# A recommender's attention pass: rows gathered straight from the embedding table instead of a prepared table of 128 columns

## The chip, the cores and the metric

One Trainium2 chip, of which the kernel uses one core. The metric is the device time of one execution in microseconds (us); lower is better. The kernel before takes 32778.58 us, the median of three runs (32776.94, 32778.58 and 32779.38 us). Engines are named as in the profile: PE is the matrix engine, DVE the vector engine, ACT the scalar engine, POOL the engine that issues the gathers, SP the engine that issues most other transfers.

## What is computed

The batch has B = 16384 samples; each has a history of L = 200 items, one candidate item, one category and one user. Rows of the embedding tables have D = 64 floats (256 bytes). All of it is 32-bit.

```
u, it, c = u_emb[user], i_emb[item], c_emb[cate]        # [B, 64] each
h = i_emb[hist]                                         # [200, B, 64]: 3.28 million rows
feat = concat([h, it, h - it, h * it])                  # [200, B, 256]
a = dice(feat @ au_W1 + au_b1, au_alpha, over the batch)# [200, B, 36]
w = a @ au_W2 + au_b2                                   # one weight per history row
cur = sum over the 200 of w * h                         # [B, 64]
z = concat([u, it, c, cur])                             # [B, 256]
z = dice(z @ W1 + b1);  z = dice(z @ W2 + b2);  out = z @ W3 + b3
```

`dice` takes mean and variance over the batch (for the attention: of each of the 200 positions by itself), and multiplies x by p + alpha (1 - p), where p is the sigmoid of the normalised x. Because the moments run over the batch, a position's weights can be formed only after all its 16384 samples have passed the first layer.

## The kernel before

The samples of one position l are cut into 128 columns of 128 samples, and the columns into ND = 8 chunks of TD = 16. One *step* k handles chunk k % 8 of position k // 8; there are 1600 steps. A step's work is spread over ten later steps, since the weights have to wait for the moments of the position.

**A prologue makes a table.** For each item it stores 128 floats in device memory: the row of `i_emb` and, beside it, the row's product with the first-layer weights (`blk_h`). `table_rows` and `table_store` do that block by block; meanwhile POOL gathers the candidate items, users and categories (384 gathers, `fetch_one`, `keep_one`); the users and categories are turned and stored to device memory (`ucT`) for the end.

**A step of the main part** (`step`, around L440) then does, in this order of issue: `fetch(k)` gathers 16 columns from the table on POOL, one gather of 128 rows of 512 bytes each (L144); an addend `xit` is loaded by SP (L344); `x_of(k-10)` goes through the sigmoid and a scaling on ACT (L423, L426); `turn(k-1)` transposes the landed rows on DVE (L354, four instructions of 64x1024); ACT copies the addend and the turned rows into PSUM (L428, L430); `hidden(k-2)` adds what the matmul made (L366) and measures it (L368); `product(k-1)` multiplies the rows with the items (L360) and multiplies by the weights `blk_m` on PE (L194, four matmuls of 512 columns); `weigh(k-10)` forms the weights by a product (L374), a transpose (L375), a reduction (L377) and three small instructions (L381, L384), multiplies the rows by them (L389) and adds to `cur` (L390). Once a position, `moments` makes mean and variance.

**One tile in 256 does not come by a gather.** In every sixteenth step (`has_side`) POOL gathers 15 columns, and the sixteenth column comes by address: SP reads 128 addresses into registers and issues one transfer of one row for each (`rows_by_address`, L332), 8 in each step, into a tile `side` that ACT copies into place (L349).

**What sets the order.** The loop (L459) has a body of LPB = 24 positions and runs 8 times; the last 8 positions follow without a loop. Each engine executes its instructions in the written order, and waits at an instruction until the others have done what it needs. `fetch(k)` overwrites the buffer of `fetch(k-12)`, so POOL waits for `weigh(k-12)`. At the end of each pass through the loop's body all engines meet.

**After the main part** the head runs by itself: the stored users and categories are loaded again (L512), the first layer takes two matrices of 80 outputs (L194 of `px`), then its dice (L528, L529, L535), the second layer, its dice, and the third layer with 256 narrow matmuls (L551) and one output transfer (L555).

Of the kernel before, what the change touches and what calls it, by code (L numbers as in the profile page):

```python
# [9 lines left out]
I32 = mybir.dt.int32  # L10
# [10 lines left out]
LPB = 24  # L21
LAND = 12
EVERY = 16
ROW = 4 * 2 * D
U8 = mybir.dt.uint8
EARLY = 4
IDX = 2
XI = 2
# [3 lines left out]
def din_kernel(  # L32
# [31 lines left out]
    Z1, Z2, ZO = W1.shape[1], W2.shape[1], W3.shape[1]  # L64

# [3 lines left out]
    dram = ctx.enter_context(tc.tile_pool(name="dram", bufs=1, space=bass.MemoryType.DRAM))  # L69
# [4 lines left out]
    def quarter(e, g, n=S):  # L74

        return slice((2 * e + g) * S, (2 * e + g) * S + n)


    eps = const.tile([P, 1], F32, name="eps")
    nc.vector.memset(eps, EPS)  # L80

    parts = [(0, S), (S, A - S)]

    blk_h = const.tile([P, P], F32, name="blk_h")
    blk_i = const.tile([P, P], F32, name="blk_i")
    blk_m = const.tile([P, P], F32, name="blk_m")
    au_w = const.tile([P, 4, A], F32, name="au_w")
    au_bias = const.tile([P, 1], F32, name="au_bias")  # L90
    au_al = const.tile([P, 1], F32, name="au_al")
    au_1al = const.tile([P, 1], F32, name="au_1al")
    au_w2 = const.tile([P, 1], F32, name="au_w2")
    au_bias2 = const.tile([P, 1], F32, name="au_bias2")
    for t in (blk_h, blk_i, blk_m, au_bias, au_al, au_w2):
        nc.vector.memset(t, 0.0)
    nc.sync.dma_start(au_bias2, au_b2.partition_broadcast(P))
    for e in range(2):
        rows = au_W1.rearrange("(g d) a -> d g a", d=D)[e * S : (e + 1) * S]
        for g in range(2):  # L100
            r = quarter(e, g)
            nc.sync.dma_start(au_w[r], rows)
            for q, (a0, n) in enumerate(parts):
                c, a = quarter(q, g, n), slice(a0, a0 + n)
                nc.vector.tensor_add(blk_h[r, c], au_w[r, 0, a], au_w[r, 2, a])
                nc.vector.tensor_sub(blk_i[r, c], au_w[r, 1, a], au_w[r, 2, a])
                nc.vector.tensor_copy(blk_m[r, c], au_w[r, 3, a])
    for g in range(2):
        for q, (a0, n) in enumerate(parts):
            r, a = quarter(q, g, n), slice(a0, a0 + n)  # L110
            nc.sync.dma_start(au_bias[r], col(au_b1)[a])
            nc.sync.dma_start(au_al[r], col(au_alpha)[a])
            nc.sync.dma_start(au_w2[r], au_W2[a])

    nc.vector.tensor_scalar(au_1al, au_al, -1.0, 1.0, ALU.mult, ALU.add)
    nc.vector.tensor_mul(au_1al, au_1al, au_w2)
    nc.vector.tensor_mul(au_al, au_al, au_w2)

    itT = const.tile([P, ND, CD], F32, name="itT")
    cur = const.tile([P, NT, D], F32, name="cur")  # L120
    nc.vector.memset(cur, 0.0)


    land = [const.tile([P, TD, 2 * D], F32, name=f"land{i}") for i in range(EARLY)]
    idx = [const.tile([P, NT], I32, name=f"idx{i}") for i in range(IDX)]

    side = [const.tile([P, 2 * D], F32, name=f"side{i}") for i in range(2)]
    addr = [const.tile([1, P], I32, name=f"addr{i}") for i in range(2)]
    stats = [const.tile([P, 2 * ND, nc.vector.BN_STATS_DIM], F32, name=f"st{i}") for i in range(2)]
    rstds = [const.tile([P, 1], F32, name=f"rs{i}") for i in range(2)]  # L130
    shifts = [const.tile([P, 1], F32, name=f"sh{i}") for i in range(2)]
    px = [psum.tile([P, CD], F32, name=f"px{i}") for i in range(2)]
    ph = psum.tile([P, CD], F32, name="ph")
    pg = psum.tile([P, CD], F32, name="pg")


    table = dram.tile([V, 2 * D], F32, name="table")
    xi = dram.tile([ND, P, CD], F32, name="xi")
    ucT = dram.tile([2, ND, P, CD], F32, name="ucT")

    def gather(dst, ids, rows):

        for n in range(ids.shape[1]):
            nc.gpsimd.indirect_dma_start(  # L144
                out=dst[:, n, :],
                out_offset=None,
                in_=rows,
                in_offset=bass.IndirectOffsetOnAxis(ap=ids[:, n : n + 1], axis=0),
            )

    def load_ids(t, ids):
        nc.sync.dma_start(t, ids.rearrange("(p n) -> p n", n=NT))

    def load_hist_ids(i, l):
        nc.sync.dma_start(idx[i], r_hist[ds(l, 1), :].rearrange("l (p n) -> p (l n)", n=NT))

    def load_addresses(m, l):

        t = addr[m % 2]
        with nc.allow_non_contiguous_dma(reason="one index of each partition"):  # L160
            nc.sync.dma_start(
                t.unsqueeze(1), r_hist[ds(l, 1), :].rearrange("l (p n) -> l n p", p=P)[:, NT - 1 :]
            )
        nc.vector.tensor_scalar_mul(t, t, ROW)  # L164

    def has_side(k):
        return k % EVERY == EVERY - 1

    def by_tile(t, i):

        return t[:, ts(i, CH)].rearrange("p (n t) -> p n t", t=S)

    def transpose(dst, rows, n=TD):

        for i in range(2):
            for e in range(2):
                nc.vector.transpose(
                    by_tile(dst[ts(e, D)], i)[:, :n], rows[ts(i, D), :n, ts(e, S)]
                )

    def transpose_back(rows, src, n=TD):

        for i in range(2):
            for e in range(2):
                nc.vector.transpose(
                    rows[ts(i, D), :n, ts(e, S)], by_tile(src[ts(e, D)], i)[:, :n]
                )

    def layer(dst, pairs, n=CH, onto=False):

        for i in range(2):
            cols = slice(i * CH, i * CH + n)
            for j, (lhsT, rhs) in enumerate(pairs):
                nc.tensor.matmul(  # L194
                    dst[:, cols], lhsT, rhs[:, cols],
                    start=(j == 0 and not onto), stop=(j == len(pairs) - 1),
                    skip_group_check=onto,
                )

    def scale_and_shift(mean, var, n, rstd=None, shift=None):  # L200

        std = small.tile([P, 1], F32, tag="std", name="std")
        nc.scalar.activation(std[:n], var, AF.Sqrt, bias=eps[:n])  # L203
        if rstd is None:
            rstd = small.tile([P, 1], F32, tag="rstd", name="rstd")
            shift = small.tile([P, 1], F32, tag="shift", name="shift")
        nc.vector.reciprocal(rstd[:n], std[:n])
        nc.vector.scalar_tensor_tensor(shift[:n], mean, -1.0, rstd[:n], ALU.mult, ALU.mult)
        return rstd[:n], shift[:n]


    with ExitStack() as start:
        pre = start.enter_context(tc.tile_pool(name="pre", bufs=3))
        ids = [start.enter_context(tc.tile_pool(name=f"ids{i}", bufs=1)).tile(
            [P, NT], I32, name=f"ids{i}") for i in range(3)]
        for t, v in zip(ids, (r_item, r_user, r_cate)):
            load_ids(t, v)
        load_hist_ids(0, 0)

        per = V // P  # L220
        rest = V - P * per
        grid = i_emb[: P * per].rearrange("(p n) d -> p n d", n=per)
        grid_out = table[: P * per].rearrange("(p n) d -> p n d", n=per)
        blocks = [(n0, min(TD, per - n0)) for n0 in range(0, per, TD)]
        if blocks[-1][1] == TD and rest:
            blocks.append((per, 0))
        tabs = {}

        def table_rows(b):

            n0, n = blocks[b]
            tab = pre.tile([P, TD, 2 * D], F32, tag="tab", name="tab")
            m = n
            if n:
                nc.sync.dma_start(tab[:, :n, :D], grid[:, n0 : n0 + n])
            if b == len(blocks) - 1 and rest:
                nc.vector.memset(tab[:, n, :D], 0.0)
                nc.sync.dma_start(tab[:rest, n, :D], i_emb[P * per :])
                m = n + 1
            rT = pre.tile([P, CD], F32, tag="rT", name="rT")  # L240
            transpose(rT, tab, m)
            layer(px[b % 2], [(blk_h, rT)], n=m * S)
            tabs[b] = tab, m

        def table_store(b):
            n0, n = blocks[b]
            tab, m = tabs.pop(b)
            transpose_back(tab[:, :, D:], px[b % 2], m)
            if n:
                nc.scalar.dma_start(grid_out[:, n0 : n0 + n], tab[:, :n])  # L250
# [335 lines left out]
```

## Time and profile before

| | us |
|---|---|
| median of three runs | 32778.58 |
| span of the profiled execution, first to last instruction | 32775.9 |
| POOL busy, 25888 instructions | 24422.0 (75% of the span) |
| DVE busy, 28939 instructions | 25619.7 (78%) |
| ACT busy, 7214 instructions | 7665.2 (23%) |
| PE busy, 7216 matmuls | 6395.0 (20%) |
| POOL's first gather begins | 9.80 |
| POOL's last gather begins | 32399.71 |

The profile is of one execution, taken by the hardware's profiler. A group's row gives the line, engine and operation, the tile written and those read, how often it ran, the busy time and the mean of one in ns, and after the second bar how long the engine was idle just before, with what ended the idle time. "issue" there means that the profile shows nothing that the engine waited for: it was the engine's own handling of the next instruction. In the timeline each row has its start, its length and, in brackets, the idle time before it. Share of busy time alone does not tell the bound: DVE and POOL have nearly the same.

### The profile page before, as it was taken

The page shows a single profiled execution, that of the slowest core. Times are in us where ns is not written, and L with a number is a line of the kernel's source. Part 1 is how long each engine was busy: PE and PEld are TensorE (multiplying, and loading weights), DVE is VectorE, ACT ScalarE, POOL GpSimd, SP SyncE. Part 2 cuts the span into 40 slices and gives each one's busy share as a digit, 9 for nine tenths or more (in the row PEclk, how much of TensorE's full clock was granted, in tenths as well). Part 3 has the DMA queues.
Part 4 walks back from the last instruction along what each step waited for, and adds up shares of the span by engine and source line. Part 5 has one row for each costly group of instructions (what it writes and reads, how often), then busy time and mean ns, then how long its engine had stood idle before and what let it go on. Part 6 is the DMA issues. An engine that isn't in the chain of part 4 may idle for free. (4 is left out here: it accounts for less than half of the span.)

```text
span 32775.9 us, 127799 instructions
## 1 busy us (share of the span) xinstructions
PE 6395.0 (20%) x7216; PEld 2044.0 (6%) x7216; DVE 25619.7 (78%) x28939; ACT 7665.2 (23%) x7214; POOL 24422.0 (75%) x25888
## 2 busy tenths in 40 slices
PE   3111111111111111111111111111111111111113
PEld 0000000000000000000000000000000000000001
DVE  7777777777777777777777777777777777777776
ACT  1222222222222222222222222222222222222222
POOL 7777777777777777777777777777777777777774
PEclk5555555555555555555555555555555555555555
DMA  5222222222222222222222222222222222222221
GB/s 157 80 80 80 80 79 80 79 80 79 80 80 80 80 78 80 80 80 80 79 80 80 79 80 80 80 80 80 79 79 80 80 80 78 80 80 79 80 80 53
DMA packets 1245023, 2650.84 MB, mean 81 GB/s; under 512 B 574678, under 2 KB 613622, under 8 KB 1237942
## 3 DMA queue, kind: packets, MB, share of 16 engines
q0 software_dynamic: 828288, 1685.41, 19.9%
q1 hardware_dynamic: 405238, 893.85, 8.8%
q10 hardware_dynamic: 10560, 63.79, 0.5%
q14 instruction: 922, 7.55, 0.1%
q8 instruction: 15, 0.25, 0.0%
HBM read 2577.29 MB, written 63.91 MB: 81 GB/s over the span
## 5 line engine op out<-in xcount | busy, mean ns | idle before, releaser
L144 POOL DMA_INDIRECT land<-table,idx x25500 | 24059.4, 944 | 7852.3 <-issue 7532.9
L354 DVE STREAM_TRANSPOSE hx<-land 64x1024 f32<-64x1024 f32 x6404 | 7938.0, 1240 | 5528.1 <-DMA land<-table,idx 5338.6
L194 PE MATMUL px<-hm,blk_m 128*128 128x512 f32 x6404 | 5974.7, 1088 | 25917.5 <-DVE hm L360 25917.5
L426 ACT ACTIVATE pg<-gate,au_al,au_1al 128x1024 f32<-128x1024 f32 x1610 | 1943.8, 1207 | 12867.9 <-DVE cur L390 12867.6
L430 ACT COPY ph<-hx 128x1024 f32<-128x1024 f32 x1601 | 1627.7, 1017 | 10549.5 <-DVE hx L354 10549.5
L194 PEld LDWEIGHTS px<-hm,blk_m 128*128 128x128 f32 x6404 | 1879.4, 324 | 30012.2 <-DVE hm L360 28357.9
L368 DVE BATCH_NORM_STATS2 st<-land 128x6 f32<-128x512 f32 x3204 | 2061.0, 685 | 55.0
L375 DVE STREAM_TRANSPOSE yT<-pg 128x1024 f32<-128x1024 f32 x1610 | 2011.8, 1250 | 55.2
L389 DVE TENSOR_TENSOR pg<-land,ph 128x1024 f32<-128x1024 f32 x1610 | 1977.7, 1228 | 54.9
L390 DVE TENSOR_TENSOR cur<-pg,cur 128x1024 f32<-128x1024 f32 x1610 | 1970.5, 1224 | 55.5
L377 DVE TENSOR_REDUCE r<-yT 128x32 f32<-128x1024 f32 x1610 | 1964.0, 1220 | 55.3
L366 DVE TENSOR_TENSOR land<-px,hx 128x1024 f32<-128x1024 f32 x1602 | 1961.6, 1224 | 49.5
L423 ACT ACTIVATE gate<-land,sh,rs 128x1024 f32<-128x1024 f32 x1610 | 1991.5, 1237 | 2.9
L374 DVE TENSOR_TENSOR pg<-pg,land 128x1024 f32<-128x1024 f32 x1610 | 1968.9, 1223 | 11.0 <-ACT pg L426 11.0
L360 DVE TENSOR_TENSOR hm<-ph,itT 128x1024 f32<-128x1024 f32 x1601 | 1932.0, 1207 | 5.6 <-ACT ph L430 5.6
L428 ACT COPY px<-xit 128x1024 f32<-128x1024 f32 x1601 | 1591.4, 994 | 31.8 <-PE px L194 22.0
L384 DVE SCALAR_TENSOR_TENSOR ph<-r,au_bias,r 64x16 f32<-64x16 f32 x3220 | 773.7, 240 | 114.8
L164 DVE TENSOR_SCALAR addr<-addr 1x128 int32<-1x128 int32 x100 | 31.2, 312 | 702.6 <-DMA addr<-in_r_hist 702.6
L423 ACT ACT_TABLE_LOAD x210 | 269.4, 1283 | 558.4 <-DMA land<-table,idx 333.0
L381 DVE COPY r<-r 64x32 f32<-64x32 f32 x1610 | 322.8, 200 | 55.0
L203 ACT ACT_TABLE_LOAD x203 | 260.4, 1283 | 3.5
L203 ACT ACTIVATE std<-var,eps 128x1 f32<-128x1 f32 x201 | 59.2, 294 | 721.0 <-DVE var L410 721.0
(79 smaller groups left out, 2102.9 us busy)
## 6 DMA issues: line engine op xcount, KB each, us to landing
xit<-xi SPq DMA_DIRECT2D x1601, 512.0 KB
land<-table,idx POOLq DMA_INDIRECT x25500, 2.5
side<-table SPq DMA_DIRECT2D x12800, 0.5 KB
table<-tab ACTq DMA_DIRECT2D x48, 1024.0 KB
tab<-in_L_rec_i_emb SPq DMA_DIRECT2D x48, 512.0 KB
idx<-in_r_hist SPq DMA_DIRECT2D x200, 64.0 KB
ucT<-t ACTq DMA_DIRECT2D x16, 512.0 KB
land<-ucT SPq DMA_DIRECT2D x16, 512.0 KB
```

Source lines behind the costliest of these rows:

```text
L144: nc.gpsimd.indirect_dma_start(out=dst[:, n, :], out_offset=None, in_=rows, in_offset=bass.IndirectOffsetOnAxis(ap=ids[:, n : n + 1], axis=0),
L194: nc.tensor.matmul(dst[:, cols], lhsT, rhs[:, cols], start=(j == 0 and not onto), stop=(j == len(pairs) - 1), skip_group_check=onto,)
L354: nc.vector.transpose(dst.rearrange("p s (n t) -> p n s t", t=S), rows[ts(i, D), :, :, e])
L366: nc.vector.tensor_add(x_of(k), by_row(px[k % 2]), by_row(hx[k % 2][:, 1]))
L368: nc.vector.bn_stats(stats[l % 2][:, 2 * c + i, :], x_of(k)[:, ts(i, TD // 2)])
L374: nc.vector.tensor_mul(by_row(pg), by_row(pg), x_of(k))
L375: nc.vector.transpose(yT, pg)
L377: nc.vector.tensor_reduce(r, yT.rearrange("p (i n u) -> p i n u", i=2, u=S), mybir.AxisListType.X, ALU.add)
L389: nc.vector.tensor_mul(by_row(pg), rows, w.unsqueeze(2).to_broadcast([P, TD, D]))
L390: nc.vector.tensor_add(cur[:, ts(c, TD)], by_row(pg), cur[:, ts(c, TD)])
L423: nc.scalar.activation(by_row(gate), x_of(k - 10), AF.Sigmoid, bias=shifts[i], scale=rstds[i])
L426: nc.scalar.activation(pg, gate, AF.Identity, bias=au_al, scale=au_1al)
```

## The change

Nothing of the result changes. What is done differently:

- **No table.** The prologue that multiplied all of `i_emb` and stored a table is gone. The gathers read `i_emb` itself, rows of 256 bytes, into `rows` (a ring of 5 tiles of 128x16x64; before, 12 of 128x16x128). The product with `blk_h` is formed in each step on PE, and the item's part too (`blk_i` with `itT`), so the addend `xit` and its transfers are gone.
- **All work in the turned layout.** `turn` transposes 64 instead of 128 floats per row into `hT` (four instructions of 64x512, as those of L177 before). The weight of a row is formed by a matmul with a matrix of ones per block (`blk_w`) that also spreads it over the row's 64 places; one instruction multiplies by the turned rows and one adds to `curT`. The transpose, reduction and small instructions of `weigh` are gone.
- **One column by address in each position.** `SIDES = (7,)`: chunk 7 of every position gathers 15 columns, and its sixteenth comes by address on SP, 16 rows in each step (25600 rows in all; before, 12800). The addresses are one contiguous load.
- **Users and categories last.** Of the 384 gathers outside of the history, 128 (items) stay at the beginning; 256 (categories and users, in turns) follow the last history gather, while the last ten steps' weighing still runs. The first layer of the head is done chunk by chunk beside these gathers (`head_layer`, from the third of these 16 steps on).
- **A new head.** Two groups of 64 samples side by side fill all 128 partitions; 64 of the 80 first-layer outputs go to `za`, the other 16 of four chunks share one tile `zb`. The third layer is 16 wide matmuls and two transposes, and eight output transfers (and one small) go out.
- **Loop.** The body holds 45 positions and runs 4 times; 20 positions follow without a loop.

The core of the diff ("..." where lines are left out):

```diff
-LPB = 24
-LAND = 12
-EVERY = 16
-ROW = 4 * 2 * D
+LPB = 45
+ROWS = 5
+LAG = 10
+XR = 9
+IDX = 3
+SIDES = (7,)
+LOAD = 16
+ROW = 4 * D
...
-    table = dram.tile([V, 2 * D], F32, name="table")
...
+    def transpose(dst, of):
+        for i in range(2):
+            for e in range(2):
+                nc.vector.transpose(by_tile(dst[ts(e, D)], i), of[ts(i, D), :, ts(e, S)])
...
+    def fetch(k):
+        l, c = divmod(k, ND)
+        for n in range(TD - has_side(k)):
+            j = column(c, n)
+            gather(rows[k % ROWS], idx[l % IDX][:, j : j + 1], n, i_emb)
+
+    def gate(k):
+        i = k // ND % 3
+        nc.scalar.activation(pg, xs[k % XR], AF.Sigmoid, bias=shifts[i], scale=rstds[i])
+        nc.scalar.activation(pg, pg, AF.Identity, bias=au_al, scale=au_1al)
+
+    def weights(k):
+        nc.vector.tensor_mul(y, pg, xs[k % XR])
+        layer(wb, [(blk_w, y)])
+
+    def weigh(k):
+        nc.vector.scalar_tensor_tensor(wb, wb, au_bias2, hT[k % LAG], ALU.add, ALU.mult)
+        nc.vector.tensor_add(curT[k % ND], wb, curT[k % ND])
+
+    def hidden(k):
+        nc.scalar.activation(xs[k % XR], px, AF.Identity, bias=au_bias)
+
+    def measure(k):
+        l, c = divmod(k, ND)
+        for i in range(2):
+            nc.vector.bn_stats(stats[l % 3][:, 2 * c + i, :], xs[k % XR][:, ts(i, CH)])
+
+    def turn(k):
+        if has_side(k):
...
+            nc.scalar.copy(rows[k % ROWS][:, TD - 1], side[m % 3])
+        transpose(hT[k % LAG], rows[k % ROWS])
+        layer(px, [(blk_h, hT[k % LAG]), (blk_i, itT[k % ND])], last=False)
+        nc.scalar.copy(ph, hT[k % LAG])
+
+    def product(k):
+        nc.vector.tensor_mul(hm, ph, itT[k % ND])
+        layer(px, [(blk_m, hm)], first=False)
...
+    def step(k, last=None):
...
+        if has(k):
+            fetch(k)
+        if has(k - LAG):
+            gate(k - LAG)
+            weights(k - LAG)
+        if has(k - 2):
+            hidden(k - 2)
+            measure(k - 2)
+        if has(k - 1):
+            turn(k - 1)
+        if has(k - LAG):
+            weigh(k - LAG)
+        if has(k - 1):
+            product(k - 1)
+        if has(k - 2) and (k - 2) % ND == ND - 1:
+            moments((k - 2) // ND)
...
+        load_ids(ids[0], r_item)
+        load_hist_ids(0, 0)
...
+        nc.gpsimd.iota(lanes, pattern=[[1, P]], base=P, channel_multiplier=-1)
+        attention_weights()
...
+        ask(-1, L)
+        head_weights()
...
+    with tc.manual_schedule():
+        steps(BODY, L - BODY, L - BODY)
+        for j in range(2 * ND + 2):
+            if j < 2 * ND:
+                head_fetch(K + j, j)
+            step(K + j, last=K - 1)
+            if 1 <= j <= 2 * ND:
+                transpose(ucT[(j - 1) % 4], rows[(K + j - 1) % ROWS])
+            if j >= 2:
+                head_layer(j - 2)
...
+        for c in range(ND + 1):
+            if c < ND:
+                dice(curT[c], za[c], na, al1a, ala)
...
+                    nc.tensor.matmul(pz[c % 4][:, cols], w2a, curT[c][:, cols], start=True, stop=False)
+                    nc.tensor.matmul(pz[c % 4][:, cols], w2b[q], ab[c // 4][q, cols], start=False, stop=True)
+            if c:
+                nc.scalar.activation(z2[c - 1], pz[(c - 1) % 4], AF.Identity, bias=bias2)
+                measure_head(2, c - 1, z2[c - 1])
```

In the built order `head_weights` (45 small transfers on SP and some small DVE work) stands, but for one memset, behind the loop, in the first two steps of the 20 positions that follow it.

## The prediction

> **What bounds the kernel now.** I read the groups first (the page's costliest groups), for the idle time as much as for the busy time.
>
> ```profile
> L144 POOL DMA_INDIRECT land<-table,idx x25500 | 24059.4, 944 | 7852.3 <-issue 7532.9
> L354 DVE STREAM_TRANSPOSE hx<-land 64x1024 f32<-64x1024 f32 x6404 | 7938.0, 1240 | 5528.1 <-DMA land<-table,idx 5338.6
> ```
>
> POOL and DVE are equally busy, but their idle times differ in kind. DVE waits 5339 us for gathered rows to land: it has time to spare. POOL's idle time is "issue": it waits for nobody, and needs about 0.3 us between gathers. Then the timeline: POOL alone around the end of a pass through the loop's body, the passage of the index load, and the last gather.
>
> ```profile
> 8147.89 0.94 POOL L144 DMA_INDIRECT land<-table,idx  x1 [0.30 <-issue]
> 8158.63 0.94 POOL L144 DMA_INDIRECT land<-table,idx  x1 [9.79 <-issue]
> ...
> 11975.98 0.94 POOL L144 DMA_INDIRECT land<-table,idx  x1 [0.30 <-issue]
> 11977.22 0.94 POOL L144 DMA_INDIRECT land<-table,idx  x1 [0.30 <-issue]
> 11987.96 0.94 POOL L144 DMA_INDIRECT land<-table,idx  x1 [9.79 <-issue]
> ...
> 32399.71 0.94 POOL L144 DMA_INDIRECT land<-table,idx  x1 [0.30 <-issue]
> ```
>
> From 8158.63 to 11977.22 lie one body's gathers, 24 x 128 less 12 = 3060, so 3059 intervals: 3818.59 / 3059 = 1.2483 us each, with no other gap. So POOL's gathers are the bound, from the first at 9.80 to the last at 32399.71: 25884 gathers (25500 and 3 x 128), 25883 intervals x 1.2483 = 32310, and the rest of the 32389.9 is 80 us of gaps. The gaps are seven turns of the loop (six of 10.74 - 1.25 = 9.5 us, the first, at 4321.87, of 6.2), 2.7 at its exit, and two waits of 9.7 and 4.4 for a buffer of the ring at 528 and 558. Preparing the table costs nothing today: it lies beside the first 384 gathers.
>
> After the last gather come 375.2 us (32400.65 to 32775.9) without POOL. The chain of waits that ended last shows what fills them.
>
> ```profile
> 32498.29 112.47 PE px L194 x256
> 32619.83 10.44 PE px L194 x12
> ...
> 32693.26 7.00 PE ph L551 x32
> 32703.63 7.00 PE pg L551 x32
> ```
>
> The ten delayed steps' weighing lasts until 32500, then follow the head's first layer (112 us), its second (until about 32690) and eight pieces of third layer, one each 10.37 us. So span = 9.8 + 32310 + 80 + 0.9 + 375.2 = 32775.9. The runs' median is 2.7 above this span, and I add 2.7 at the end.
>
> **The change, part by part.** *Price of a gather.* It reads 256 bytes instead of 512 per row, from `i_emb`, into a tile of 64 columns. The trace of before has such gathers: those of its prologue.
>
> ```profile
> L144 POOL DMA_INDIRECT land<-in_L_rec_i_emb,ids x128 | 120.9, 944 | 48.0 <-issue 38.1 <-DMA ids<-in_r_item 9.3 <-DMA land<-in_L_rec_i_emb,ids 0.6
> L144 POOL DMA_INDIRECT land<-table,idx x25500 | 24059.4, 944 | 7852.3 <-issue 7532.9 <-DMA land<-table,idx 123.1 <-DVE yT L375 66.4
> ```
>
> 944 ns for 64 columns, 944 ns for 128; issue 38.1 / 127 = 0.30 us in both. Halving the bytes gains POOL nothing and costs it nothing. The users' group of the same prologue has 128 gathers with 120.8 busy and 39.0 idle: 159.8 / 128 = 1.2484. I take 1.2483, and 0.001 to either side as bounds, so +-25 us.
>
> *Number of gathers.* 200 x 127 + 3 x 128 = 25784, which is 100 fewer: 100 x 1.2483 = -125 us. Intervals: 25783 x 1.2483 = 32185.
>
> *What must now keep up with POOL*, which needs 16 x 1.2483 = 19.97 us for a step. DVE, by rows of before: product for the weights 1.22 (L374), measuring 2 x 0.685 (L368), four 64x512 transposes x 0.706 = 2.82 (L177), weighing 2 x 1.22 (L389, L390 the nearest), product 1.21 (L360): 9.1 us against about 16.0 (25619.7 / 1600) before. ACT: 1.24 + 1.21 + 1.11 + 1.02 = 4.6. PE: eight matmuls x 1.09 = 8.7. In series from landing: transposes 2.8, weighing 2.4, product 1.2, two matmuls 2.2, ACT 1.1, measuring 1.3 = 11 us. None reaches 19.97, so the 7 us per step that DVE saves gain nothing, and the matmuls added cost nothing: POOL's issue hides them. `fetch(k)` now waits for the turning of k-5 instead of the weighing of k-12. POOL feels it only where a `turn` comes later than four steps of issue, 80 us, less landing and turning (1.64 from the last gather's end to L354 at the end of before, and 2.8): 75 us of cover. Behind a late gather the next turn waits, and behind that nobody who isn't already waiting. The two ring waits at 528 and 558 go (ring now freed after turning): -14, between -14 and 0.
>
> *Rows by address* on SP: 128 for each position instead of 64.
>
> ```profile
> 496.97 48.66 SPq L332 DMA_DIRECT2D side<-table  x124
> 552.32 2.73 SPq L332 DMA_DIRECT2D side<-table  x8
> 556.48 2.87 SPq L332 DMA_DIRECT2D side<-table  x8
> ```
>
> 124 rows in 48.66 us, register loads and all, are 0.39 us a row; in the loop 8 rows, an addend load and a register load take 4.16 us, at most 0.52 a row. So 50 to 67 us of SP's 158.5 us per position (127 x 1.2483), and the addend loads are gone. SP starts a position's rows eight steps before use, and the last 16 rows two steps before. Past them on SP's queue move the index load, the address load and, once, head_weights' 45 transfers (x 0.4 = 18 us, behind the loop); each is wanted no sooner than four steps (80 us) later, and the DVE instructions that wait on those 45 have the 75 us cover. Nothing, then. Here a rule speaks against the change: the Trainium skill, "DMA: Bandwidth & Descriptors", section "Anatomy of one DMA", gives a DMA a fixed cost of about 2 us whatever its size (stated for the path that POOL uses). If SP paid that in series, a position would take 128 x 2 = 256 us, SP would be the bound and the kernel would take 200 x 256 = 51200 us. The row says 0.39: the fixed part overlaps among transfers. I go by the row.
>
> A second rule: the skill, "SBUF — State Buffer", section "SBUF: two separate sides", says that a DVE instruction in a 2-port mode locks POOL out of writing descriptors, so that its DMAs wait until DVE is done. In the timeline near 15003 (DVE busy without pause) and 15013 (DVE idle for 7 us) the gathers have the same 0.94 and 0.30. DVE's forms after are those of before except the weighing's scalar_tensor_tensor, which has its output in PSUM. By the row: 0. By the rule, if that one form locked: up to 1600 x 1.2 = +1920 us.
>
> *Loop.* Three turns instead of seven: 3 x 9.5 + 2.7 at the exit = 31 us of gaps, between 25 and 45 (the body is longer; what an edge costs after it no row shows). With the ring waits gone, gaps go from 80 to 31.
>
> *Start.* The ids come first on SP. Before, the ids' transfer was issued at 7.84 and the first gather began at 9.80, so 2 us later; now issue at about 0.8 gives 2.8. POOL has an iota before it that no row shows: nearest are its own memsets, 0.1 us, and DVE's 128x128 memset, 0.17. I take a start at 4; bounds 2.8 and 12 (iota of 9 us).
>
> *After the last gather.* Users' gather lands and is turned: 1.6 + 2.8. Its first layer: four matmuls 4, ACT 1.1, measuring 1.3, so 11 us with hops. Two chains of moments: 3 each (of before: 32613.2 to 32615.0, with two more small matmuls), so 17. Table load 1.3, two dice (1.24, 0.8, 1.22) for `zb` and the first for `za`: 25. Second layer: four matmuls x 0.86 = 3.4 per chunk, DVE 0.8 + 1.22 + 1.29 = 3.3 per chunk; they alternate at about 3.8, so 8 x 3.8 = 31 and 3 for the last ACT and measuring: 59. Moments and table load 5: 64. Third: eight dice x 2.02 of DVE = 16, a transpose and two sums 1.7 twice, the last two matmuls 1.7, output 4 x 0.4 and 2.5 to land: 90. I take 90 against 375.2; bounds 75 and 120. The first layer and the ten steps' weighing lie beside the 256 gathers at the end; if that cover were gone, their 98 and 112 us come back, about 300.
>
> Sum: 4 + 32185 + 31 + 0.9 + 90 = 32311 span, + 2.7 = **32314 us**, 1.4% less: -125 gathers, -49 gaps, -6 start, -285 end.
>
> **The rivals.** *A, the tail isn't hidden.* The head's first layer needs `curT` complete; if weighing runs late it follows the gathers as before, with 200 to 300 us at the end: about 32480. Against it: DVE has 9 us of work in 20. *B, POOL waits once per position for the side column*, since chunk 7 now comes by address in each: a few us x 200; with 1 us 32514. It needs a `turn` 75 us late. *C, slower: POOL's gathers get dearer* through the weighing instruction's hold on the shared port (place: every step; price up to its 1.2 us). It decides from 465 / 25784 = 0.018 us per gather, 0.29 us per step; at half its length per step the result is 32314 + 960 = 33274. Against it: sixteen gathers a step at a constant 1.25 beside every form of before. *D, the gain is given back exactly* would need C's price at 0.29: hardly.
>
> **How the numbers follow.** Mine 0.87, A 0.03, B 0.04, C 0.05, D 0.01. My case's own range from the bounds (gathers +-25, gaps -6 to +14, start -1 to +8, end -15 to +30, not all at once) is 32275 to 32370, nine times in ten: 0.78. To hold 8 in 10 I go to 32270 and 32390. A measurement tells 0.2% (66 us) from no change; faster are mine, A and B: 0.94; same 0.01; slower 0.05.
>
> **What would show it.** POOL's gathers at 944 ns and 0.30 us apart, 25784 of them, idle mostly by "issue"; DVE busy about 14600 us and waiting longer for landing; SP's rows near 0.4 us; three gaps of about 10 us; a first gather before 5 us; 75 to 120 us after the last one. I am wrong if the interval isn't 1.248, if POOL waits on DVE, or if the end is longer.

## The result, and the profile after

The changed kernel takes **32351.83 us** (median of four runs, 32349.32 to 32352.71); the kernel before took 32778.98 beside it (four runs, 32776.94 to 32779.74). The ratio is 0.987, with a 95% interval of 0.9856 to 0.9884: 1.3% faster. The forecast was 32314 with a range of 32270 to 32390. The profiled execution has a span of 32350.9 us. This holds for a chip on which the kernel before takes 32779 us. Three other chips came up in the experiments, on which the kernel before needs 15% more; there all variants of the change that were run are slower than the kernel before, as the experiments tell. In the text TensorE is the profile's PE, VectorE its DVE, ScalarE ACT, GpSimd POOL and SyncE SP; the granted clock is the share of full speed at which TensorE's clock ran.

The costliest groups of the kernel after, with the row of the new weighing instruction and the count of each engine (columns: busy us, mean ns of one, idle us before, what ended most of it):

```profile
PE 15634.4 (48%) x26020; PEld 6232.0 (19%) x26020; DVE 14906.8 (46%) x18956; ACT 7799.0 (24%) x7281; POOL 24330.4 (75%) x25789
...
L117 POOL DMA_INDIRECT rows<-in_L_rec_i_emb,idx x25400 | 23967.5, 944 | 7767.4 <-issue 7296.0
L146 DVE STREAM_TRANSPOSE hT<-rows 64x512 f32<-64x512 f32 x6404 | 4519.2, 706 | 12357.6 <-DMA rows<-in_L_rec_i_emb,idx 11955.0
...
L286 DVE SCALAR_TENSOR_TENSOR wb<-wb,au_bias,hT 128x1024 f32<-128x1024 f32 x1610 | 2080.9, 1292 | 82.6 <-PE wb L151 30.4
```

DVE fell from 25619.7 to 14906.8 us, and what it saved became waiting: for landing rows it now waits 11955 us, 5339 before. POOL has the same 944 ns and the same kind of idle time, "issue". It is still the bound. The timeline of POOL, at the start and at one of the loop's edges (the end of a pass through its body):

```profile
0.86 0.22 POOL L379 IOTA lanes<- 128x128 int32 x1 [0.40 <-POOLq L538]
2.83 1.09 POOL L117 DMA_INDIRECT rows<-in_L_rec_i_emb,ids  x1 [1.75 <-DMA ids<-in_r_item]
...
14434.25 0.94 POOL L117 DMA_INDIRECT rows<-in_L_rec_i_emb,idx  x1 [0.30 <-issue]
14445.07 0.94 POOL L117 DMA_INDIRECT rows<-in_L_rec_i_emb,idx  x1 [9.87 <-issue]
```

The iota took 0.22 us, inside the wait for the ids. In the whole trace only four intervals between gathers are longer than 1.4 us: 4.88 at 7296, 10.82 at 14434 and at 21579, 3.72 at 28723. The two ring waits of before are gone. Less four normal intervals that makes 25.2 us of gaps.

The last gather ends at 32216.88, and the span at 32350.93: 134 us. The chain of work that ended last, in order of time (start, length, what), shows what fills them:

```profile
32215.93 2.31 DMA rows<-in_L_rec_u_emb,ids
...
32243.65 2.04 PE px L488 x2
32245.70 2.00 PE px L489 x2
...
32319.68 9.58 PE px L151 x16
...
32333.06 9.70 PE pg L151 x16
```

From 32243.65 to 32307.8 TensorE works on the second layer (L488, L489) without pause: 64 us. The third layer is the two pieces of 16 matmul instructions at L151. Stretches of this end by engine (columns: stretch, length, busy us and instructions of PE, PEld, DVE, ACT, POOL, then the granted clock, the DMA share and GB/s):

```profile
32235.00:32260.00 25.00, 16.34 (x17) 4.35 (x18) 11.11 (x12) 8.35 (x8) 0.00 (x0) 0.50 0.00 1
32260.00:32310.00 50.00, 47.80 (x48) 11.63 (x47) 18.44 (x24) 13.19 (x12) 0.00 (x0) 0.50 0.00 0
32310.00:32351.00 41.00, 20.39 (x36) 8.79 (x36) 20.62 (x29) 12.21 (x11) 0.00 (x0) 0.67 0.02 3
```

In the second row TensorE is busy 47.80 of 50 us at a granted clock of 0.50, with 48 instructions: 1.00 us each.

### The profile page after: what moved, and what is told of

The parts are those of the page before. It is cut to its first block, busy times and chain, and to the rows that moved or that the text cites. A ratio compares the mean times of both kernels' runs of the same rounds, so it can differ in the third digit from the quotient of the medians.

```text
span 32350.9 us, 170467 instructions
## 1 busy us (share of the span) xinstructions
PE 15634.4 (48%) x26020; PEld 6232.0 (19%) x26020; DVE 14906.8 (46%) x18956; ACT 7799.0 (24%) x7281; POOL 24330.4 (75%) x25789
## 5 line engine op out<-in xcount | busy, mean ns | idle before, releaser
L117 POOL DMA_INDIRECT rows<-in_L_rec_i_emb,idx x25400 | 23967.5, 944 | 7767.4 <-issue 7296.0
L151 PE MATMUL px<-hT,blk_h 128*128 128x512 f32 x6404 | 5638.3, 979 | 15307.4 <-DVE hT L146 15307.4
L146 DVE STREAM_TRANSPOSE hT<-rows 64x512 f32<-64x512 f32 x6404 | 4519.2, 706 | 12357.6 <-DMA rows<-in_L_rec_i_emb,idx 11955.0
L151 PEld LDWEIGHTS px<-hT,blk_h 128*128 128x128 f32 x6404 | 1808.7, 313 | 18318.3 <-issue 17505.7
L151 PE MATMUL px<-itT,blk_i 128*128 128x512 f32 x6404 | 4721.2, 830 | 0.0
L151 PE MATMUL wb<-y,blk_w 128*128 128x512 f32 x6440 | 3412.6, 656 | 1253.6 <-DVE y L282 1253.6
L295 DVE BATCH_NORM_STATS2 st<-xs 128x6 f32<-128x512 f32 x3204 | 2058.3, 684 | 3695.9 <-ACT xs L290 3695.9
L151 PE MATMUL px<-hm,blk_m 128*128 128x512 f32 x6408 | 3037.0, 596 | 38.9 <-DVE hm L382 35.0
L151 PEld LDWEIGHTS px<-itT,blk_i 128*128 128x128 f32 x6404 | 1853.6, 289 | 2849.6 <-issue 2849.6
L282 DVE TENSOR_TENSOR y<-pg,xs 128x1024 f32<-128x1024 f32 x1610 | 1955.1, 1214 | 740.2 <-ACT pg L279 740.0
L286 DVE SCALAR_TENSOR_TENSOR wb<-wb,au_bias,hT 128x1024 f32<-128x1024 f32 x1610 | 2080.9, 1292 | 82.6 <-PE wb L151 30.4
L287 DVE TENSOR_TENSOR curT<-wb,curT 128x1024 f32<-128x1024 f32 x1610 | 1971.3, 1224 | 54.8
L151 PEld LDWEIGHTS wb<-y,blk_w 128*128 128x128 f32 x6440 | 1307.0, 207 | 2985.2 <-issue 1542.1
L151 PEld LDWEIGHTS px<-hm,blk_m 128*128 128x128 f32 x6408 | 1190.7, 190 | 1691.3 <-issue 1233.3
```

Of the source, the lines that this page charges most:

```text
L117: nc.gpsimd.indirect_dma_start(out=dst[:, n, :], out_offset=None, in_=table, in_offset=bass.IndirectOffsetOnAxis(ap=ids, axis=0),)
L146: nc.vector.transpose(by_tile(dst[ts(e, D)], i), of[ts(i, D), :, ts(e, S)])
L151: nc.tensor.matmul(dst[:, ts(i, CH)], lhsT, rhs[:, ts(i, CH)], start=(first and j == 0), stop=(last and j == len(pairs) - 1), skip_group_c ...
L282: nc.vector.tensor_mul(y, pg, xs[k % XR])
L286: nc.vector.scalar_tensor_tensor(wb, wb, au_bias2, hT[k % LAG], ALU.add, ALU.mult)
L287: nc.vector.tensor_add(curT[k % ND], wb, curT[k % ND])
```

## Experiments

The first theory: POOL's gathers set the time, 1.2484 us for each, and beyond them only the end counts. The rival: something of the new steps (the column by address, VectorE, the shorter ring) is part of the price. The first four kernels ran on a chip where the kernel before took 32778.97.

**The column by address taken out.**

```
-SIDES = (7,)
+SIDES = ()
...
```

("...": the loads and issues for such a column are skipped where there is none.)

> Undo one part: no column by address, all 128 columns of a position are gathered on POOL (200 gathers more, SP's 25600 single-row transfers gone). My theory (POOL's issue of gathers sets the time, the column by address costs nothing beside it): 200 x 1.2484 = +250 us on the changed kernel's 32352, so 32602, interval between gathers still 1.248. Rival (the column by address makes POOL or DVE wait once per position, so part of what it saves is lost): less than +250, nearer to the changed kernel.

Measured: 32590.01 us (32586.76 to 32621.16; the longest one was profiled, with 1.2496 us from gather to gather). That is 238 more than the change as it is. 200 further gathers x 1.2484 are 249.7; the gaps at the loop's edges are 7 us smaller, and the end behind the last gather 129 us in place of 134, which brings the 249.7 to 238. The column by address is worth what its gathers cost POOL, and nothing else, within these few us. So of the 427 us that the whole change gains, 189 come without it.

**Two columns by address.**

```
-SIDES = (7,)
+SIDES = (3, 7)
```

> The same part, one step further: two columns of each position by address (chunks 3 and 7), 256 rows of SP per position. My theory: 200 gathers fewer, -250 us, so 32102, as long as SP's 256 rows at 0.39 to 0.52 us (100 to 133 us) fit into POOL's 126 x 1.2484 = 157 us. Rival (SP is nearly the bound already): above 32352, POOL or DVE waiting for the rows of SP, from 0.61 us a row.

Measured: 32121.15 us (two runs, 32102.88 and 32139.41; in the profiled, longer one each gather's interval was 1.2499). The waits of SyncE (what waited for what, total us, times, longest), first of the change as it is, then of this kernel:

```profile
SPq L258 <- DVE y L282: 20693.4, 198, 131.7
```

```profile
SPq L258 <- DVE y L282: 10042.0, 195, 77.8
```

SyncE's spare time falls by 10651 us for 25600 more rows, in a span that is 213 us shorter, so a row costs 0.41 us there (10438 / 25600). POOL still waits for nobody. On this chip the step is linear: a column by address takes 200 gathers out.

**VectorE given three times the transposes.**

```
-        transpose(hT[k % LAG], rows[k % ROWS])
+        for _ in range(3):
+            transpose(hT[k % LAG], rows[k % ROWS])
```

> Adds work: the four transposes of a step are done three times, which gives DVE 8 x 0.706 = 5.6 us more per step (about 9000 us in all), nearly what the change took off it. My theory (DVE's saving gained nothing, its work lies beside POOL's issue): the same time within 10 us, 32345 to 32365, DVE's wait for landed rows shorter by the 9000 us. Rival (part of the gain came from a less busy DVE): up to 300 us more, towards the kernel before.

Measured: 32352.42 us (32352.16 and 32352.68), no change. The groups:

```profile
L117 POOL DMA_INDIRECT rows<-in_L_rec_i_emb,idx x25400 | 23966.3, 944 | 7768.2 <-issue 7338.8
L146 DVE STREAM_TRANSPOSE hT<-rows 64x512 f32<-64x512 f32 x19212 | 13558.3, 706 | 3385.1 <-DMA rows<-in_L_rec_i_emb,idx 2046.3
```

VectorE got 9033 us more work (23939.8 busy), its wait for landing rows shrank from 11955 to 2046, and POOL's row stayed as it was. So what the turned layout saves on VectorE is worth nothing here by itself.

**The second layer's weights at full height.** In the changed kernel the matmuls of L489 read 32 rows of `w2b` and of `ab`, those of one group of chunks. Here they read all 128, with zeros in the rows that don't count; the result is the same, and the number of matmuls too.

```
-    w2b = make("w2b", P, P)
+    w2b = make("w2b", P, 4, P)
...
-                    nc.tensor.matmul(pz[c % 4][:, cols], w2b[q], ab[c // 4][q, cols], start=False, stop=True)
+                    nc.tensor.matmul(pz[c % 4][:, cols], w2b[:, c % 4], ab[c // 4][:, cols], start=False, stop=True)
```

> The head's second layer alone: the matmuls of 32 rows (w2b) become matmuls of all 128 rows, with zeros in the rows that don't count; their number stays. In the changed kernel this layer takes 64 us after the last gather, 64 matmul instructions one after the other, 1.00 us each at a granted clock of 0.50. Theory 1 (matmuls that use a quarter of the rows keep the granted clock low): the clock rises above 0.6 there, an instruction costs 0.43 to 0.6 us, the layer takes 32 to 40 us and the whole 25 to 32 us less, 32320 to 32327. Theory 2 (the clock is low there for another reason, the number of instructions sets the price): 32352 again, clock 0.50.

Measured: 32319.33 us (32318.73 and 32319.92), 32.5 less than the change as it is, and the fastest one here with one column by address. TensorE's timeline, first with 32 rows, then with 128:

```profile
32243.65 2.04 PE L488 MATMUL px<-curT,w2a 128*128 128x512 f32 x2 [9.47 <-issue]
32245.63 2.07 PE L489 MATMUL px<-ucT,w2b 32*128 32x512 f32 x2
```

```profile
32246.63 1.02 PE L487 MATMUL ph<-curT,w2a 128*128 128x512 f32 x2
32247.49 1.02 PE L488 MATMUL ph<-ucT,w2b 128*128 128x512 f32 x2
...
32259.64 1.10 PE L487 MATMUL px<-curT,w2a 128*128 128x512 f32 x2 [1.16 <-ACT itT L490]
```

and the windows of this kernel over its second layer (columns as above):

```profile
32235.00:32260.00 25.00, 17.04 (x33) 7.04 (x34) 17.39 (x21) 11.06 (x11) 0.00 (x0) 0.79 0.00 1
32260.00:32290.00 30.00, 18.10 (x40) 7.56 (x39) 18.90 (x28) 17.20 (x16) 0.00 (x0) 0.83 0.00 0
```

The clock is granted at 0.79 to 0.83 instead of 0.50, two instructions (one call) take 0.86 us in place of 2.0, and the layer takes 34.5 us. TensorE is no longer its bound, and no other engine is: TensorE is busy 18.1 and VectorE 18.9 of the 30 us, and they wait in turn (TensorE 1.16 us before every second chunk). The end behind the last gather shrinks from 134 to 101.6 us, which is within the bounds of the forecast's 90 (75 to 120). So the matmuls of 32 rows hold the clock down here; whether by having 32 rows, or by the change between 32 and 128, no run tells. If an instruction's time goes with the clock, 0.50 makes 0.86 us of the 0.43 measured at 0.99 in the first layer of the kernel before; where the other 0.14 us of the 1.00 come from is open.

**On other chips.** The remaining eight runs came to three further chips. There the kernel before took 37918.9 us (second chip), 37687.3 (third) and 37621.5 (fourth) instead of 32779, so each is only compared with the kernel before on its own chip, which was timed there and not profiled. Most of their expectations were worked out for the first chip, and miss by the chip. The changed kernel itself did not run on these three.

*Four columns by address, and a ring of four*, second chip:

```
-ROWS = 5
+ROWS = 4
...
-SIDES = (7,)
+SIDES = (1, 3, 5, 7)
```

> Four columns of each position by address (chunks 1, 3, 5, 7), 512 rows of SP per position, and a ring of four tiles of rows instead of five to make room. In the run with two columns SP waited 10042 of 32138 us for others and issued 51200 rows in the rest, about 0.41 us a row. My theory (SP's cover ends where its rows need more than POOL's gathers): 512 x 0.41 = 211 us per position against 124 x 1.2484 = 155, so SP becomes the bound, about 200 x 211 + 200 = 42500 us (40000 to 53500 for 0.39 to 0.52 a row), with POOL waiting on what waits for SP. Rival (POOL's issue stays the bound, rows cost SP less than 0.30 us when nothing holds it up): 32352 - 600 x 1.2484 = 31603.

Measured: 67627.79 us. The waits:

```profile
ACT rows L301 <- DMA side<-in_L_rec_i_emb: 46253.3, 796, 62.8
...
DVE hT L146 <- ACT rows L301: 38608.9, 796, 61.8
POOL rows L117 <- DVE hT L146: 35372.6, 785, 47.3
```

ScalarE waits for nearly every one of the 800 columns, VectorE for ScalarE, POOL for VectorE: SyncE has become the bound, as expected, but the whole divided by its rows is 67626 / 102400 = 0.66 us in place of 0.41.

*A ring of two tiles*, second chip:

```
-ROWS = 5
+ROWS = 2
```

> The ring of landed rows has 2 tiles instead of 5. My theory (a turn comes 4 to 5 us after its rows' last gather, while POOL needs 20 us for the next tile): no wait added, 32352 within 10 us. Rival (turns come late now and then, at a position's end or at the column by address, and the ring's depth hides it): POOL waits for DVE's transposes, 1 us or more per position, 32550 or more.

Measured: 38591.36 us, 1.018 times the kernel before there. POOL waits 6274.5 us for transposes, but with the ring of five it waits as long (6233.5 in the next kernel, on the same chip), so no wait of a shorter ring is seen here, and how it would go on the first chip stays open.

*The 256 category and user gathers left out* (the output lacks their part), second chip, and the same kernel again on the third:

```
-            gather(rows[k % ROWS], ids[1 + u][:, i : i + 1], n, (c_emb, u_emb)[u])
+            pass
```

> Leaves out the 256 gathers of categories and users after the last history gather (old rows stand in for them; the output is not the reference's). All other work stays, so what these gathers cover comes into the open: the last ten steps' weighing and the head's first layer (16 pieces, 256 matmul instructions of 0.43 to 1.0 us, 110 to 256 us). My theory: 256 x 1.2484 = -320, and 110 to 250 uncovered, so 32140 to 32280, the time after the last gather 250 to 380 instead of 134. Rival (they covered next to nothing, the end is as long as before anyway): 32032 to 32060.

> The 256 gathers of the category and user rows are left out, so the output lacks their part. If the tail behind the last gather is what it was (134 us, set by TensorE's layers and not by what the late gathers deliver), only 256 to 257 intervals of 1.2484 us go: -320, so 32030 to 32060 us. Rival: the late gathers cover work of the attention steps that still runs when the last item row lands; then that work comes out behind the last gather and the time falls by less, to 32080 to 32280 us, with a tail above 150 us.

Measured: 38481.03 us on the second chip (1.015 times before), 38905.55 on the third (1.032). The totals are ruled by waits that come further down. But the end can be read by itself: behind the last gather come 330.9 us on the second chip and 335.9 on the third, where the change has 134. From the chain of work on the second chip, where the last gather ends at 38146.27:

```profile
38206.43 6.35 PE px L151 x12
...
38352.89 1.85 PE ph L151 x4
```

The weighing of the last steps ends 149 us after the last gather, and the head's first layer 208 us after it; in the change the weighing ends 147 us before the last gather does and the first layer 10 us after it. No stretch of half a microsecond in the second chip's end is without work on TensorE, VectorE or ScalarE. So the theory of the first expectation holds for the end (250 to 380), and the rival of the second one (above 150): the 256 late gathers cover about 199 us of work. On the first chip, leaving them out would then save some 120 us of their 320, an estimate that was not measured.

What rules the total are POOL's waits, third chip:

```profile
POOL rows L117 <- issue: 7548.9, 24302, 54.8
POOL rows L117 <- DVE hT L146: 6597.4, 523, 19.7
```

POOL's interval is the old one wherever it doesn't wait (1.2484 us over the 24946 intervals below 1.4 us), but 523 times it waits for a transpose, about 12.6 us each. Of that wait the change has none on the first chip.

*Each gather takes 64 rows in place of 128* (half of each tile's rows stay zero, so half of the output is missing), second chip:

```
-            out=dst[:, n, :],
+            out=dst[: P // 2, n, :],
...
-            in_offset=bass.IndirectOffsetOnAxis(ap=ids, axis=0),
+            in_offset=bass.IndirectOffsetOnAxis(ap=ids[: P // 2], axis=0),
```

> Each gather fetches 64 rows instead of 128 (the other half of each tile stays zero; the output is not the reference's), the number of gathers is the same. If POOL's price is per row, a gather takes half of 0.944 and the same 0.30 between: 0.77 us, a step 12.4 us, and with DVE's 9.1 us and the chain of 11 us from landing just below it the whole takes about 20000 us. If the price is per gather, 32352 as before. If half of it is fixed: 1.01 us, 26200.

Measured: 38827.62 us (one run), with the same kind of waits. Between the waits its timeline can be read:

```profile
15024.53 0.90 POOL L117 DMA_INDIRECT rows<-in_L_rec_i_emb,idx  x1 [0.30 <-issue]
...
15039.02 0.90 POOL L117 DMA_INDIRECT rows<-in_L_rec_i_emb,idx  x1 [0.30 <-issue]
```

The twelve intervals from 15024.53 to 15039.02 are 14.49 / 12 = 1.2075 us each. 64 rows fewer save 0.041 us of 1.248: a gather of 64 rows costs nearly what one of 128 does. Of the three prices expected, the one per gather holds.

*Two columns by address, the second layer at full height, and a loop body of 90 positions*, together, third and fourth chip:

```
-LPB = 45
+LPB = 90
...
-SIDES = (7,)
+SIDES = (3, 7)
...
```

("...": the second layer's weights as in the experiment above.)

> Two sides from SyncE, the second layer's weights at full height, and loop bodies of twice the length, together. If the three terms are separate parts of the sum (200 gathers fewer at 1.2484 us: -249.7; the second layer at full height: -32.5 as measured alone; fewer loop edges, each some 9.6 us above a normal interval: -10 to -20), the time is 32050 to 32085 us. Rival: the terms do not add, because with twice the rows SyncE comes late or the longer body makes another engine wait: then it stays above 32110 us and GpSimd shows waits on VectorE's transposes of some tens of us.

> Two sides from SyncE, the second layer's weights at full height, and loop bodies of twice the length, together, once more. On a chip where the kernel before takes some 32779 us: 32050 to 32085 us if the three terms add, above 32110 us if they don't. On a chip where the kernel before takes 37600 to 37900 us: again some 46900 us, set by SyncE's issue of the rows by address.

Measured: 46921.07 us (1.245 times before there, 1.2429 to 1.2472) and 46847.37 (1.245). The first expectation, made for the first chip, is missed by 14800 us. What its rival named is what the waits show: SyncE comes late and POOL waits for transposes, for 14687 us and not some tens. The second expectation held for its chip. The waits on the third chip:

```profile
POOL rows L117 <- DVE hT L146: 14687.1, 783, 44.9
ACT rows L301 <- DMA side<-in_L_rec_i_emb: 13224.7, 398, 53.6
```

398 of the 400 columns by address come late, by 33 us each. SyncE itself waits for others in only 958 of its 46905 us, where on the first chip a third of its time is left. The whole divided by rows is 0.92 us here, 0.66 with four columns, and 1.52 with one (38908 / 25600, late gathers left out, third chip), though in that run only 21 columns come late. So the quotient isn't the price of a row. Half of the rows here and with four columns are issued within 0.33 us of the one before, as on the first chip; others take several times as long, and why stays open. On the first chip the sum of the terms measured one by one would be 32352 - 250 - 32.5 = 32070, less 10 to 20 for the loop, an estimate; it was not measured.

*The column by address taken out, again*, fourth chip (diff as at the first experiment):

> The column fetched by address taken out again, so all rows come by GpSimd's gathers. On a chip where the kernel before takes some 32779 us: 32587 to 32602 us, as before. On a chip where the kernel before takes 37600 to 37900 us there are two theories. If the rows by address on SyncE (25600 issues, which nearly double the instructions that have to be loaded) make the loss there, this one comes out below the kernel before, at 37000 us or less. If the loss comes from the rest of the change (the turned layout's shorter steps, more instructions on TensorE, ScalarE and VectorE), it stays above the kernel before, at 38000 to 38900 us.

Measured: 38192.82 us, 1.015 times before there (1.0096 to 1.0204). The second theory holds: with no row by address at all the change is slower than before on such a chip, by 1 to 2%, so this loss is in the rest of it. On the first chip the same kernel was 0.6% faster than before (32590 against 32779). Its waits ("remote" and "issue" both stand for time that the profile ties to no other engine's work):

```profile
ACT xs L294 <- remote: 16638.1, 712, 36.2
...
PE px L155 <- issue: 8539.9, 1155, 33.1
...
POOL rows L117 <- DVE hT L150: 5496.0, 400, 22.3
```

POOL's 5496 us of waits are the difference to the same kernel on the first chip (38193 - 32590 = 5603) but for 107. They go back to pauses of ScalarE and TensorE of up to 36 us each. On TensorE these come at recurring numbers of instructions: with the late gathers left out, third chip, 492 of the 544 distances between pauses (starts over 15 us apart) are exactly 48 matmul instructions, which are three steps; the change on the first chip has six such pauses in all. One could think of the loading of the instructions themselves, but two readings speak against it. The packets of the queue that loads them (8192 bytes each) took 0.445 us there and 0.433 on the first chip, so their transfer isn't slower; and in 330 of those 545 pauses no such packet starts at all. The cause stays open. So does what the kernel before pays there: it loses 4843 us against the first chip (37621 - 32779), nearly as much as this one's 5603.

## Why the prediction was right, and where it was off

| term of the sum | predicted, us | measured, us |
|---|---|---|
| first gather begins | 4 (2.8 to 12) | 2.83 |
| 25783 intervals between gathers | 32185 (1.2483 each) | 32188 (1.2484 each) |
| gaps | 31 (25 to 45) | 25.2 |
| the last gather itself | 0.9 | 0.9 |
| after the last gather | 90 (75 to 120) | 134.0 |
| runs' median over the span | 2.7 | 0.9 |
| sum | 32314 | 32352 |

- **The price of a gather** (no gain from half the bytes, no loss) held: 1.2484 us. The run with 64 rows adds that half of the rows count for 3% of it.
- **The number of gathers** held, and the two runs with no column and with two columns show that each column moves the time by its 200 gathers.
- **"What must now keep up with POOL"** held on this chip: VectorE tripled in its transposes costs nothing, and POOL does not wait for a transpose. VectorE's busy time was predicted at 14600 and is 14906.8; the new weighing instruction takes 1292 ns, where the nearest row said 1220.
- **TensorE** was counted too low, without harm: "eight matmuls x 1.09 = 8.7" per step. Each call of 512 columns of 32-bit numbers shows as two instructions in the trace, and 1.09 (1088 ns, L194 before) is the mean of one instruction, so calls were multiplied by the price of an instruction. A step has 16 instructions, now at 0.60 us on average (15634.4 / 26020), and TensorE is busy 15634 / 1600 = 9.8 us of a step's 19.97. Two errors nearly cancelled here.
- **Rows by address** near 0.4 us: 0.41 by the second experiment. The 2 us that the Trainium skill ("DMA: Bandwidth & Descriptors", section "Anatomy of one DMA") gives for one DMA, on the path that POOL uses, are not paid in series on SyncE's queue.
- **The weighing's hold on the shared port** (rival C): nothing. POOL's interval is 1.2485 us in the 1954 intervals that the weighing instruction (L286) covers for 0.6 us or more, and 1.2484 in the 22559 that it doesn't touch.
- **The step that failed is the size of the end**, in "After the last gather": "Second layer: four matmuls x 0.86 = 3.4 per chunk", alternating with VectorE's 3.3 at 3.8, hence 31 us. The count is right: four calls, that is, eight instructions. The price is not. 0.86 us is what a call (two instructions of 0.43) takes in the head's first layer of the kernel before, at a granted clock of 0.99 (first row below). In the second layer of the change a call takes 2.0 us at a clock of 0.50, so a chunk takes 8.0 us and the layer 64, with TensorE as its pace. With 128 rows throughout a call is at the predicted 0.86 again, and the layer takes 34.5 us, close to the 31. A nearer price was there to be read: the second layer of the kernel before (second row, and its group) ran at 0.50 too, with matmuls of 80 rows.

```profile
32500.00:32613.00 113.00, 110.75 (x255) 38.38 (x253) 41.77 (x65) 18.84 (x17) 0.00 (x0) 0.99 0.15 47
32632.00:32690.00 58.00, 44.18 (x50) 7.76 (x48) 40.98 (x55) 31.43 (x29) 0.00 (x0) 0.50 0.00 0
L194 PE MATMUL px<-a,w 80*40 80x512 f32 x64 | 56.3, 1058 | 15.6 <-DVE a L535 10.6 <-ACT z L505 5.0
```

  Its 64 instructions are 32 calls in 56.3 us, 1.76 us each; with that price the sum would have had 4 x 1.76 x 8 = 56 us in place of 31. Of the 44 us by which the end came out longer than predicted (14 beyond its upper bound), 33 are this layer. About 9 more are the third layer, 35 us in place of 26: the prediction had VectorE as its pace and 1.7 us for the last two matmuls, but VectorE waits for TensorE's 16 matmul instructions twice, 3.7 and 3.9 us. The start and the gaps (7 us less together) and the median's distance (1.8 less) gave back a little, and the intervals added 3, so that the total is 38 us high. It is inside the range because the end is a small part of the sum, and not because the end was understood.
- **Rivals A, B, D** did not occur on the chip of the result: the weighing ends beside the late gathers, and there is no wait once per position. The "about 300" us that the prediction gave for an end without that cover is borne out by the two runs without the late gathers, with 331 and 336 us behind the last one. On the other three chips what happens is nearest to B, in that POOL waits for transposes, though it comes 400 to 785 times in 200 positions, also where there is no column by address, and with pauses of TensorE and ScalarE that the forecast did not have among its cases.

## What to carry to other kernels

Where one engine issues back to back and waits for nobody, count its instructions and multiply: bytes, rows and other engines' savings don't enter until one of them comes near its period. Price what you count: a matmul call of 32-bit numbers is two instructions in the trace here, so an instruction's mean and a call's time differ by a factor of two. Look at the granted clock of a short exposed stage before pricing it by a row from another stage. And time a change on more than one chip: the kernel without a column by address was 0.6% faster than before on one chip and 1.5% slower on another, and two columns by address gained 2% on one and lost 25%, in a kernel with two further changes, on others.

## What the runs showed that was not expected

- With matmuls of 32 rows between matmuls of 128 rows the granted clock stays at 0.50 (1.00 us for an instruction of 512 columns); padded to 128 rows with zeros, the same number of instructions run at 0.79 to 0.83, 0.43 us apart. The padding saved 32.5 us of the kernel's time.
- An indirect gather on POOL costs 1.248 us for 128 rows, whether of 512 or of 256 bytes, and 1.2075 us for 64 rows: between these two, 0.64 ns a row.
- The same program differs by 15% between chips (32779 and 37600 to 37900 us for the kernel before; 32590 and 38193 for the change without a column by address). In the second pair the interval of gathers that don't wait is the same, 1.25 us; what the slower chip adds are pauses of 15 us and more on TensorE, VectorE and ScalarE, 749 on TensorE in place of six.
- 256 gathers at the end of the main part cover some 199 us of weighing and of the head's first layer, which come into the open when the gathers are left out.
